# Four early sampling blocks in attention, weights by axis, denser background calls, and a second addition formed by TensorE in a four-layer image network

## The chip, the cores and the metric

The kernel runs on one core of one Trainium2 chip. The metric is the device time of one launch in microseconds (us); lower is better. Names of engines below: PE is TensorE, DVE is VectorE, ACT is ScalarE, POOL is GpSimd, SP is SyncE, which only issues DMAs here.

## The reference

The input x is 2 images of 256 channels on 64 x 64 pixels, float32. Four layers follow one another:

```
# layer 0: attention over 4096 pixels, 4 heads of 64 channels
xn = group_norm(x, groups=8)
q, k, v = split(w_qkv @ xn)
out = softmax(q^T k / 8) @ v
x = xn + w_proj @ out + b_proj
# layer 1: a position term is added
x = x + pe(W, b)
# layer 2: bottleneck with a modulated deformable 3x3 convolution on 64 channels
h = relu(bn1(w1 @ x))
off = conv3x3(h, woff) + boff            # 18 offsets and 9 masks per pixel
h = einsum(bilinear(h, y + off, x + off) * sigmoid(mask), w2)
x = relu(bn3(w3 @ relu(bn2(h))) + x)
# layer 3: two deformable 3x3 convolutions on 256 channels
h = relu(group_norm(x, groups=32))
off = pw1 @ depthwise7x7(h)              # 18 offsets per pixel
h = einsum(bilinear(h, y + off, x + off), w1)
h = relu(group_norm(h)) ; the same again with dw2, pw2, w2
return h + x
```

`bilinear` reads for each pixel and each of 9 taps the four corners around a fractional position and weighs them; the four weights are products of two weights along y and two along x.

## The kernel before, in words

All arithmetic is float32. An image is cut into 8 blocks of 512 pixels (8 rows); pixels lie on partitions, in 4 groups of 128, where samples are made. There are two large stages, `attention` and `deform`.

**The order.** The order on PE, ACT, DVE and POOL is the order in which the program issues instructions; each engine works its own list in order. SP's DMAs are issued in order as well, and one that waits for a semaphore holds those behind it. An indirect DMA (L848) is issued by POOL: 128 rows, one per partition, at addresses from an index column.

**Attention.** Four units (batch 0 heads 0-1, batch 0 heads 2-3, batch 1 likewise) of 256 counts `n`, 1024 counts in all; one turn of the main loop handles two counts: scores on PE (L580), row maxima on DVE (L592), exponentials on ACT (L598), turns on PE (L610), copies on DVE and ACT, products with v (L639). 16 counts make a `Block` of 256 query pixels. Its own steps (`compare`, `raised`, `weights`, `spread`, `combine`, `fetch`, `project`) fall due at fixed counts and run from `small(n)` and `small(n + 1)`. `combine` (L519 to L527) runs on POOL and reads the single buffer `o`, which `product` (L471, on DVE) fills again for the next block.

**Work beside attention.** `back` is a list of generators that `background(count)` advances: from unit 1 the bottleneck's first half of batch 0 (`before(0)`), from unit 2 `first_batch` (`last(0)`, `conv(0)`, then `early_image`), from unit 3 `before(1)`, put at the front, and `early_samples`. A generator that yields something true uses up one call; one that yields False gives the call to the next. There is one call at the end of each turn, and one in each `small` that has no step of its own, from unit 2 on.

`conv(b)` is the second layer of the bottleneck: 8 blocks of 18 steps. A step makes two indirect gathers (`bfour`), weighs them with four products of weights on DVE (L1067), and adds in two goes (L1077, L1078), on POOL for batch 0 and on DVE for batch 1. After 4 steps (or 2 for the ninth tap) the sums are turned on PE (L1088) and copied by ACT (L1090); `second` and `third` are its products with w2 and w3. A step uses two calls.

`early_samples` makes the first `EARLY` = 2 blocks of samples of layer 3 for batch 0 while attention still runs: `offsets` (products L805, L825, L839, then `corners`), then 36 gathers a block from the image in DRAM, each of which is stored into `samp_d` (L1261). `self.sample` does at most one store and one gather a call; the main loop calls it 11 times in 16 counts. Its buffers are tiles of attention's pools.

**Deform.** Four layers of 288 steps `s` (batch 0 and 1 of the first deformable convolution, then of the second); a block has 36 steps (9 taps x 4 groups of 128 pixels). Step s issues the gather for s + 8, and for the first `EARLY` blocks of the first layer a plain load from `samp_d` instead, on SP's queue (L1448). Steps come in two forms:

- by axis (`paired`): ACT scales two corners with one weight (`left`, L1471), DVE adds the other two (`right`, L1477), ACT scales (`first`, L1486), DVE adds (`others`, L1490). The weights are `w`, two per axis.
- by corner: ACT scales one corner (L1486), DVE adds three (three of L1496). The weights are `w4`, four per tap.

In the first layer the early blocks go by corner and the others by axis; in the other three layers every second step goes by axis.

Then PE turns the sample (L1508), ACT copies four of them (L1517), and PE multiplies with the weights (L1527). Beside it, generators are paced by `Side(start, rate, steps, more)`: it advances while its count is below rate x (s - start) + more(s). `seconds` runs `conv(1)`; `last` the offsets of the last two blocks of batch 1; `offs` the offsets of the next blocks; `images` the image of the next layer, which begins for batch 1 when `seconds` has ended.

Of the kernel before, what the change touches and what calls it, by code (L numbers as in the profile page):

```python
# [11 lines left out]
F32 = mybir.dt.float32  # L12
# [8 lines left out]
P = 128  # L21
# [3 lines left out]
CM = 64  # L25
# [1 line left out]
EPS = 1e-5  # L27
DWK = 7

EARLY = 2  # L30


GH, GW = H + 1, W + 2
# [31 lines left out]
class Net:  # L65
# [115 lines left out]
    def attention(self, bott):  # L181
# [5 lines left out]
        with ExitStack() as ctx:  # L187
# [489 lines left out]
            while n < last + 4 or back or more or any(own.values()):  # L677
                u, d = divmod(n, per_unit)
                if d == 0 and u < len(units):
                    plan_unit(u)  # L680
                    if u == 0:
                        back.append(prepare(1))
                    if u == 1:
                        back.append(bott.before(0, bt, ps))
                    if u == 2:
                        back.append(first_batch())
                    if u == 3:
                        back.insert(0, bott.before(1, bt, ps))
                        back.append(self.early_samples(bott, bt, held, xp, vp, kp, ps))

                def small(at):
                    steps = own.pop(at, ())
                    for f in steps:
                        f()
                    if not steps and u > 1:
                        background(1)

                if n - 1 in pts:
                    p = pts.pop(n - 1)
                    keep(n - 1, p, "ACT")  # L700
                    keep(n - 1, p, "DVE")
                ps.flush()
                sc = [scores(m) for m in (n + 2, n + 3) if m < last]
                for m in range(len(sc)):
                    lowest(n + 2 + m, sc[m])
                if n < last:
                    p = turn(e.pop(n))
                    keep(n, p, "DVE")
                if sc:
                    e[n + 2] = exponentials(n + 2, sc[0])  # L710
                if n < last:
                    keep(n, p, "ACT")

                small(n)
                if 4 <= n < last + 4:
                    attend(n - 4)
                    attend(n - 3)
                small(n + 1)
                if n < last:
                    pts[n + 1] = turn(e.pop(n + 1))  # L720
                if sc:
                    e[n + 3] = exponentials(n + 3, sc[1])
                if u or n % 8 == 0:
                    background(1)

                for _ in range(1 + (n % 16 in (10, 12, 14))):
                    more = self.sample()
                n += 2


    def corners(self, i, pt, mask, base, idx, w4, pool, w=None):

        nc = self.nc
        p = pool.tile([P, 4, K2, 2], F32, name="pos")
        off = pt[:, :, 0 : 2 * K2].rearrange("p j (k t) -> p j k t", t=2)
        nc.vector.tensor_tensor(p, off, base[:, 4 * i : 4 * i + 4], ALU.add)
        if mask:
            mk = pool.tile([P, 4, K2], F32, name="mask")  # L740
            nc.vector.tensor_scalar_max(mk, pt[:, :, 2 * K2 : 3 * K2], -87.0)
        yield False
        if mask:

            nc.scalar.activation(mk, mk, AF.Exp, scale=-1.0)

        nc.vector.tensor_scalar(p, p, float(H), -1.0, ALU.min, ALU.max)
        whole = pool.tile([P, 4, K2, 2], I32, name="whole")
        nc.vector.tensor_copy(whole, p)
        yield True  # L750
        f = pool.tile([P, 4, K2, 2], F32, name="floor")
        nc.vector.tensor_copy(f, whole)
        g = pool.tile([P, 4, K2, 2], F32, name="above")
        nc.vector.tensor_tensor(g, f, p, ALU.is_gt)
        yield False
        nc.vector.tensor_tensor(f, f, g, ALU.subtract)
        nc.vector.tensor_scalar_min(f, f, float(H - 1))
        if w is None:
            w = pool.tile([P, 2, 4, K2, 2], F32, name="wt")
        nc.vector.tensor_tensor(w[:, 1], p, f, ALU.subtract)  # L760
        yield False
        nc.vector.tensor_scalar(w[:, 0], w[:, 1], -1.0, 1.0, ALU.mult, ALU.add)
        at = g.rearrange("p j k t -> p (j k t)")[:, : 4 * K2]
        at = at.rearrange("p (j k) -> p j k", k=K2)
        nc.vector.scalar_tensor_tensor(
            at, f[:, :, :, 0], float(GW), f[:, :, :, 1], ALU.mult, ALU.add
        )
        nc.vector.tensor_scalar_add(idx, at, float(GW + 1))
        yield True
        if mask:  # L770
            nc.vector.tensor_scalar_add(mk, mk, 1.0)
            nc.vector.reciprocal(mk, mk)
            yield False
            for s in range(2):
                nc.vector.tensor_mul(w[:, s, :, :, 1], w[:, s, :, :, 1], mk)
            yield False
        for s in range(4):
            nc.vector.tensor_mul(w4[:, :, :, s], w[:, s % 2, :, :, 0], w[:, s // 2, :, :, 1])
        yield True

# [75 lines left out]
    class Bottleneck:  # L856
# [3 lines left out]

        GROUPS = [(0, 1), (2, 3), (4, 5), (6, 7), (8,)]

        CORNERS = NB + EARLY + 1

        def __init__(self, ctx, net):
            self.net = net
# [31 lines left out]
            self.od = wp.tile([P, 512], F32, name="bod")  # L898
            nc.gpsimd.memset(self.od, 0.0)

        def pools(self, ctx, gathers=5, sums=8):
            self.ahead = gathers - 1
            tc = self.net.tc
            return self.kept | {
                n: ctx.enter_context(tc.tile_pool(name=f"bt_{n}", bufs=bufs))
                for n, bufs in (("g", gathers), ("s", sums), ("t", 6), ("x", 2))
            }
# [135 lines left out]
        def conv(self, b, pools, ps):  # L1043
# [28 lines left out]
            def add(n, four, sampled):  # L1072

                i, g, js = steps[n]
                engine = (nc.gpsimd, nc.vector)[b]
                sm = pools["s"].tile([P, 2, CM], F32, name="bsmp")
                engine.tensor_add(four[:, :, 0:2, :], four[:, :, 0:2, :], four[:, :, 2:4, :])  # L1077
                engine.tensor_add(sm, four[:, :, 0, :], four[:, :, 1, :])  # L1078
# [5 lines left out]
            def transpose(g, sampled):  # L1084
                n = CM * len(self.GROUPS[g])
                pt = ps([P, 512])
                for j, sm in enumerate(sampled):
                    nc.tensor.transpose(pt[:n, j * P : (j + 1) * P], sm[:, :n], net.ident)  # L1088
                st = pools["t"].tile([P, 512], F32, name="bst")
                ps.later(lambda: nc.scalar.copy(st[:n], pt[:n]))  # L1090
                return st
# [122 lines left out]
                        nc.sync.dma_start(dst, t[64 * r : 64 * r + 64])  # L1214
                yield True

    def early_samples(self, bott, pools, held, xp, vp, kp, ps):


        nc, a = self.nc, self.a  # L1220
# [26 lines left out]
        for cb in range(2):  # L1247
# [2 lines left out]
            wf.append(t[:, : T * 2 * K2].rearrange("p (t o) -> p t o", o=2 * K2))  # L1250
            self.filters(wf[cb], cb, dw, pw)
            yield True
        free = deque(x.rearrange("p u n -> p (u n)") for x in xbs)
        gathers, stores = deque(), deque()

        def gather():


            if len(stores) > 1 and len(free) < 3 or not gathers and stores:
                dst, four = stores.popleft()  # L1260
                nc.sync.dma_start(dst, four)  # L1261
                free.append(four)
# [7 lines left out]
        self.sample = gather  # L1270
        for i in range(EARLY):
            idx = bott.corner.tile([P, 4, K2], I32, name="bidx")
            w4 = self.early[i] = bott.corner.tile([P, 4, K2, 4], F32, name="bw4")
            steps = self.offsets(
                i, xs,
                lambda s, row: wf[s][:, DWK * row : DWK * row + DWK, :].rearrange(
                    "p t o -> p (t o)"
                ),
                self.vec[:, V_PWB : V_PWB + 1],
                bott.base, idx, w4, pools["work"], wide, ps,  # L1280
                odp=lambda: pools["t"].tile([P, 512], F32, name="bst"), y0=rows(i)[0],
                later=ps.later,
            )
            mine = False
            for done in steps:
# [15 lines left out]
    def deform(self, bott):  # L1301
# [5 lines left out]
        with ExitStack() as ctx:  # L1307
# [90 lines left out]
                        yield  # L1398

            IMAGE = 4 + 6 * NB + 1  # L1400
            corners = {(0, 0, i): (None, w4, None) for i, w4 in self.early.items()}

            def offsets(b, l):
                if b == 0:
# [1 line left out]
                wf = self.wf  # L1406
                for i in range(EARLY if (b, l) == (0, 0) else 0, NB):
                    idx = cp.tile([P, 4, K2], I32, name="didx")
                    w4 = cp.tile([P, 4, K2, 4], F32, name="dw4")
                    w = cp.tile([P, 2, 4, K2, 2], F32, name="dwt")  # L1410
                    corners[b, l, i] = idx, w4, w
                    yield from self.offsets(
# [44 lines left out]

            def paired(s):
                n, i, _, j = parts(s)
                return s < ALL and (i >= EARLY if n == 0 else j % 2 == 1)  # L1460

            def share(s, side, axis):
                n, i, k, j = parts(s)
# [77 lines left out]
            def finish(n, i, ob, s):  # L1541
# [14 lines left out]
                        lambda: nc.vector.bn_stats(stats[b][:, ob, i, :], xs)  # L1556
                    )
                else:
                    res = work.tile([P, 512], F32, name="res")
                    nc.sync.dma_start(res, self.x2d[b][rows, cols])  # L1560

                    def second_layer():
# [18 lines left out]
                            self.steps = None  # L1581

            OFFS = 24
            inner = ExitStack()
            second = bott.conv(1, bott.pools(inner, 8, 7), ps)
            for s in range(AHEAD):
                gather(s)
# [3 lines left out]
            next(begun)  # L1591
            load(0, self.xn_d[0], wp)
            offs = [Side(EARLY * BLOCK - LEAD - 6, OFFS / BLOCK, begun)]
            first(0)


            last = Side(0, 1, bott.last(1, bott.kept, ps))
            seconds = Side(0, 0.9, second, lambda s: 2.5 * min(s, EARLY * BLOCK))
            stats[0] = self.norm_stats()
            images = []  # L1600
            for s in range(ALL + 16):
# [15 lines left out]
                if seconds:  # L1617
                    seconds.follow(s)
                    if not seconds.steps:
                        seconds = None  # L1620
                        stats[1] = bott.stats[1]
                        inner.close()
                        images.append(Side(s, 0.9, image(*layers[1])))
                if s % LAYER == LAYER // 2 and 1 <= n < len(layers) - 1:
                    images.append(
# [111 lines left out]
```

## Time and profile before

| what | value |
|---|---|
| median of 3 runs | 5122.12 us (5121.92 to 5128.18) |
| the profiled run | 5119.31 us, its span 5117.5 us, mean granted clock 0.972 |
| busy over the span | PE 4793.9 us (94%), DVE 4025.2 (79%), ACT 3251.1 (64%), POOL 2325.6 (45%) |
| indirect gathers | 1080 of `four` and 576 of `bfour` on POOL |
| stores into samp_d, loads from it | 72 and 72 of 512 KB |
| DMA | 997.68 MB, 195 GB/s over the span |
| attention | from the start to about 2985 us |
| deform | 2985 us to the end |

The page gives for each engine its busy time and, in 40 slices of 128 us, its share in tenths. A line of the groups names the source line, engine, operation, output and input, then busy time and mean duration of one, then the idle time of the engine just before these instructions and what ended it. A line of the windows gives, for a stretch of time, the busy time of PE, weight loads (PEld), DVE, ACT and POOL with counts, the granted clock of PE, the DMA share and GB/s. In a timeline the columns are start, duration, engine, line, operation and count.

### The profile page before, as it was taken

Reading aid. Unit: us, or ns where it says so; the run is one execution under the profiler, and the core shown is the slowest. Engines: PE = TensorE matmul, PEld = TensorE weight load, DVE = VectorE, ACT = ScalarE, POOL = GpSimd, SP = SyncE. Lnnn points to the kernel's source line nnn. Section 1 sums busy time; section 2 is a strip of 40 time slices with the busy share of each in tenths; the row PEclk is TensorE's granted clock in tenths of the full one; section 3 lists DMA queues with packets and bytes.
Section 4 is the critical chain, followed back from the end, with each engine's and each line's share of the span. In section 5 each row is a group of like instructions: output and inputs, shape, how many; then the busy total and the mean of one; then the engine's idle time right before and its main releaser. Section 6 shows DMA issues by size and latency. Waiting matters only on the chain. (4 is left out here: it accounts for less than half of the span.)

```text
span 5117.5 us, 100364 instructions
## 1 busy us (share of the span) xinstructions
PE 4793.9 (94%) x38200; PEld 2669.1 (52%) x38200; DVE 4025.2 (79%) x7281; ACT 3251.1 (64%) x5869; POOL 2325.6 (45%) x2256
## 2 busy tenths in 40 slices
PE   8999999999999999999999956678999999999998
PEld 5555565555565555565555523334444444444444
DVE  6878867878768888677767668867788888888888
ACT  5676656666666666666656622247876766666666
POOL 0111111111106777565123257775777666666665
PEclk9999999999999999999999977779999999999999
DMA  5231121111112333332547767679999999999998
GB/s 173 61 97 53 43 69 49 35 47 31 55 53 80 103 98 105 93 86 70 164 147 284 274 223 236 202 237 349 358 339 352 363 376 358 366 396 344 349 352 331
DMA packets 367025, 997.68 MB, mean 195 GB/s; under 512 B 61372, under 2 KB 98810, under 8 KB 366542
## 3 DMA queue, kind: packets, MB, share of 16 engines
q0 software_dynamic: 196560, 690.41, 37.4%
q1 hardware_dynamic: 169438, 300.73, 18.0%
q8 instruction: 300, 4.92, 0.4%
q14 instruction: 183, 1.50, 0.1%
q10 hardware_dynamic: 544, 0.13, 0.0%
HBM read 855.36 MB, written 127.35 MB: 192 GB/s over the span
## 5 line engine op out<-in xcount | busy, mean ns | idle before, releaser
L598 ACT ACTIVATE e<-sc,low 128x1024 f32<-128x1024 f32 x1024 | 1146.2, 1119 | 742.3 <-DVE low L592 738.0
L848 POOL DMA_INDIRECT four<-img,didx x1080 | 1152.6, 1067 | 549.9 <-issue 140.3
L592 DVE TENSOR_REDUCE low<-sc 128x1 f32<-128x1024 f32 x1024 | 1205.0, 1218 | 231.7 <-PE sc L580 227.3
L1527 PE MATMUL out<-st,wc 128*128 128x512 f32 x2304 | 1224.8, 614 | 85.7 <-ACT st L1517 41.5
L580 PE MATMUL sc<-k,qs 64*128 64x512 f32 x2048 | 999.1, 606 | 0.5 <-DVE k L368 0.3
L639 PE MATMUL av<-et,v 128*64 128x256 f32 x8192 | 997.7, 386 | 0.0
L580 PE MATMUL sc<-k,q 64*128 64x512 f32 x2048 | 978.2, 605 | 0.0
L519 POOL TENSOR_TENSOR o<-o,f 128x1024 f32<-128x1024 f32 x63 | 149.5, 2373 | 1765.2 <-DMA f<-share_d 1007.7
L610 PEld LDWEIGHTS tt<-ident,e 64*128 64x128 f32 x16384 | 655.3, 139 | 512.9 <-issue 272.7
L629 ACT COPY et<-tt 128x512 f32<-128x512 f32 x1152 | 658.4, 584 | 171.8 <-PE tt L610 170.8
L610 PE MATMUL tt<-ident,e 64*128 64x64 f32 x16384 | 728.0, 227 | 36.3 <-ACT et L629 17.7
L627 DVE COPY et<-tt 128x512 f32<-128x512 f32 x896 | 612.5, 684 | 161.5 <-PE tt L610 160.9
L1496 DVE SCALAR_TENSOR_TENSOR smp<-four,dw,smp 128x256 f32<-128x256 f32 x1296 | 627.2, 484 | 140.5 <-ACT smp L1486 109.0
L639 PEld LDWEIGHTS av<-et,v 128*64 128x64 f32 x8192 | 554.0, 137 | 300.9 <-issue 48.4
L848 POOL DMA_INDIRECT bfour<-img,bidx x576 | 584.1, 1014 | 183.9 <-issue 94.8
L1508 PEld LDWEIGHTS pt<-ident,smp 128*128 128x128 f32 x2304 | 330.5, 144 | 633.9 <-issue 470.9
L1471 ACT ACTIVATE four<-four,dwt 128x512 f32<-128x512 f32 x648 | 465.0, 718 | 200.1 <-DMA four<-img,didx 196.6
L1477 DVE SCALAR_TENSOR_TENSOR four<-four,dwt 128x512 f32<-128x512 f32 x648 | 484.9, 748 | 112.6 <-ACT four L1471 110.2
L1527 PEld LDWEIGHTS out<-st,wc 128*128 128x128 f32 x2304 | 390.9, 196 | 339.3 <-issue 222.8
L580 PEld LDWEIGHTS sc<-k,qs 64*128 64x128 f32 x2048 | 346.9, 189 | 208.7 <-issue 116.8
L1508 PE MATMUL pt<-ident,smp 128*128 128x128 f32 x2304 | 448.8, 278 | 4.6 <-DVE smp L1496 3.1
L805 PE MATMUL pd<-x,wf 128*126 128x512 f32 x840 | 436.0, 601 | 0.0
(189 smaller groups left out, 4743.1 us busy)
## 6 DMA issues: line engine op xcount, KB each, us to landing
f<-share_d SPq DMA_DIRECT2D x128, 256.0 KB
four<-samp_d SPq DMA_DIRECT2D x64, 512.0 KB
xb<-xn SPq DMA_DIRECT2D x55, 512.0 KB
img<-imgt SPq DMA_DIRECT2D x96, 256.0 KB
four<-img,didx POOLq DMA_INDIRECT x1080
xa<-res SPq DMA_DIRECT2D x32, 512.0 KB
samp_d<-xb SPq DMA_DIRECT2D x32, 512.0 KB
xb<-in_x SPq DMA_DIRECT2D x20, 512.0 KB
```

What stands on the lines that cost most here:

```text
L580: nc.tensor.matmul(s[:, j, :], lhsT=q[u, i // 2][int(h != j)][halves[j], at : at + P], rhs=k[u][c][halves[j], h, :], start=True, stop=True,)
L592: nc.vector.tensor_reduce(low, s, AX.X, ALU.max, negate=True)
L598: nc.scalar.activation(e.rearrange("p j n -> p (j n)"), s, AF.Exp, bias=blk.low[:, g, c : c + 1], accum_out=blk.sum[:, g, c : c + 1],)
L610: nc.tensor.transpose(pt[:, m, :], e[half, m // 4, m % 4 * P : m % 4 * P + P], self.ident[half, half],)
L627: nc.vector.tensor_copy(dst, pt)
L629: nc.scalar.copy(dst, pt)
L639: nc.tensor.matmul(now["av"][halves[h], :], lhsT=v[u][c][:, m, halves[h]], rhs=ets[j][:, m, h, :], start=(m == 0), stop=(m == 7),)
L848: self.nc.gpsimd.indirect_dma_start(out=dst, out_offset=None, in_=img, in_offset=bass.IndirectOffsetOnAxis(ap=idx, axis=0),)
L1477: nc.vector.scalar_tensor_tensor(uv, four[:, 2 * C :], share(s, 1, 1), uv, ALU.mult, ALU.add)
L1496: nc.vector.scalar_tensor_tensor(smps[s], four[:, c], weight(s, c), smps[s], ALU.mult, ALU.add)
L1508: nc.tensor.transpose(pts[u][:, c, j * P : (j + 1) * P], smp[:, c * P : c * P + P], self.ident,)
L1527: nc.tensor.matmul(outs[ob], lhsT=wc[k][:, c, ob * P : ob * P + P], rhs=sts[u][:, c, :], start=(k == 0 and c == 0), stop=(k == K2 - 1 and ...
```

## The change

Attention makes four early blocks instead of two, with a fifth buffer for them (the tile `pos` of attention's pool of single buffers), and the calls of `background` and `sample` come more often. The early blocks keep their weights by axis (`w` in place of `w4`), so that the whole first deform layer takes the form by axis, and its `w4` is not made. In `conv(1)` the second addition is dropped on DVE: the one addition left writes a permuted tile, and PE turns its two halves by plain products with the identity that accumulate in PSUM, where there was one transpose. The pacing of `conv(1)` in deform is 2.0 calls a step over the first 144 steps instead of 3.4 over 72. The rest makes room or follows: tiles of `corners` are shared, the pool of sums has 7 buffers instead of 8, `res` gets its pool when that of `conv(1)` has ended, and `left` and `right` of the first steps are issued ahead of the loop.

```diff
-EARLY = 2
+EARLY = 4
...
-                        background(1)
+                        background(1 + (n % 4 == 0))
...
-                for _ in range(1 + (n % 16 in (10, 12, 14))):
+                for _ in range(1 + (n % 16 in (2, 6, 10, 12, 14))):
                     more = self.sample()
...
-        whole = pool.tile([P, 4, K2, 2], I32, name="whole")
+        whole = pool.tile([P, 4, K2, 2], F32, name="whole").bitcast(I32)
...
-        g = pool.tile([P, 4, K2, 2], F32, name="above")
+        g = whole.bitcast(F32)
...
-        for s in range(4):
+        for s in range(4 if w4 is not None else 0):
             nc.vector.tensor_mul(w4[:, :, :, s], w[:, s % 2, :, :, 0], w[:, s // 2, :, :, 1])
...
-        CORNERS = NB + EARLY + 1
+        CORNERS = NB + EARLY
...
-        def pools(self, ctx, gathers=5, sums=8):
+        def pools(self, ctx, gathers=5, sums=7):
...
                 engine = (nc.gpsimd, nc.vector)[b]
+                if b == 1:
+                    sm = pools["s"].tile([P, 2, 2, CM], F32, name="bsmp")
+                    engine.tensor_add(
+                        sm.rearrange("p s n f -> p n s f"), four[:, :, 0:2, :], four[:, :, 2:4, :]
+                    )
+                    if g < 4:
+                        sampled.append(sm.rearrange("p s n f -> p s (n f)"))
+                    else:
+                        sampled.extend(sm[:, :, m, :] for m in range(2))
+                    return
...
-                    nc.tensor.transpose(pt[:n, j * P : (j + 1) * P], sm[:, :n], net.ident)
+                    dst = pt[:n, j * P : (j + 1) * P]
+                    if b == 0:
+                        nc.tensor.transpose(dst, sm[:, :n], net.ident)
+                        continue
+                    for m in range(2):
+                        nc.tensor.matmul(
+                            dst, lhsT=sm[:, m, :], rhs=net.ident, start=(m == 0), stop=(m == 1)
+                        )
...
+        xbs.append(one.tile([P, 2, 512], F32, name="pos"))
...
-            if len(stores) > 1 and len(free) < 3 or not gathers and stores:
+            if len(stores) > 1 and len(free) < 4 or not gathers and stores:
...
-            w4 = self.early[i] = bott.corner.tile([P, 4, K2, 4], F32, name="bw4")
+            w = bott.corner.tile([P, 4, K2, 4], F32, name="bw4").rearrange("p a k c -> p (a k c)")
+            w = self.early[i] = w.rearrange("p (s j k t) -> p s j k t", s=2, j=4, t=2)
...
-            corners = {(0, 0, i): (None, w4, None) for i, w4 in self.early.items()}
+            corners = {(0, 0, i): (None, None, w) for i, w in self.early.items()}
...
-                    w4 = cp.tile([P, 4, K2, 4], F32, name="dw4")
+                    w4 = cp.tile([P, 4, K2, 4], F32, name="dw4") if b or l else None
...
-                return s < ALL and (i >= EARLY if n == 0 else j % 2 == 1)
+                return s < ALL and (n == 0 or j % 2 == 1)
...
-                    res = work.tile([P, 512], F32, name="res")
+                    res = places["res"].tile([P, 512], F32, name="res")
...
+            for s in range(3):
+                left(s)
+            for s in range(2):
+                right(s)
             first(0)
...
-            seconds = Side(0, 0.9, second, lambda s: 2.5 * min(s, EARLY * BLOCK))
+            seconds = Side(0, 0.9, second, lambda s: 1.1 * min(s, EARLY * BLOCK))
...
                         inner.close()
+                        places["res"] = ctx.enter_context(tc.tile_pool(name="df_r", bufs=2))
```

More of the change, by code (lines that the diff above doesn't have):

```diff
@@ L688, in attention @@
                         back.insert(0, bott.before(1, bt, ps))
-                        back.append(self.early_samples(bott, bt, held, xp, vp, kp, ps))
+                        back.append(self.early_samples(bott, bt, held, xp, vp, kp, one, ps))
                 def small(at):
@@ L1215, in early_image, with early_samples @@
                 yield True
-    def early_samples(self, bott, pools, held, xp, vp, kp, ps):
+    def early_samples(self, bott, pools, held, xp, vp, kp, one, ps):
         nc, a = self.nc, self.a
@@ L1279, in early_samples @@
                 self.vec[:, V_PWB : V_PWB + 1],
-                bott.base, idx, w4, pools["work"], wide, ps,
+                bott.base, idx, None, pools["work"], wide, ps,
                 odp=lambda: pools["t"].tile([P, 512], F32, name="bst"), y0=rows(i)[0],
-                later=ps.later,
+                later=ps.later, w=w,
             )
@@ L1583, in deform @@
             OFFS = 24
-            inner = ExitStack()
+            inner, places = ExitStack(), {}
             second = bott.conv(1, bott.pools(inner, 8, 7), ps)
```

## The prediction

> **What bounds the kernel now.** I read part 2 of the page first, to see where TensorE is not full, then the busy times of that stage and its neighbours, then the groups inside the stage, then single instructions for prices.
>
> ```profile
> PE   8999999999999999999999956678999999999998
> POOL 0111111111106777565123257775777666666665
> PEclk9999999999999999999999977779999999999999
> ```
> Each digit is 128 us. PE is full in attention (to 2985 us) and from about 3480 us on. The hole is the opening of the deform stage, and there POOL has its highest digits.
>
> ```profile
> 1555.00:2110.00 555.00, 544.97 (x5884) 325.26 (x5882) 459.20 (x627) 373.60 (x699) 408.28 (x450) 1.00 0.33 97
> 2985.00:3484.00 499.00, 322.57 (x1002) 151.87 (x1002) 395.15 (x899) 166.26 (x294) 373.62 (x362) 0.76 0.73 240
> 3484.00:3757.00 273.00, 257.99 (x950) 129.36 (x951) 205.36 (x425) 225.22 (x392) 183.42 (x159) 0.98 0.94 351
> 3757.00:5117.00 1360.00, 1301.58 (x4746) 644.34 (x4744) 1185.25 (x2619) 927.11 (x1612) 900.51 (x856) 1.00 0.96 358
> ```
> Columns: busy PE, PEld, DVE, ACT, POOL, clock, DMA share, GB/s. Counting the one ACT scale per step (L1486: 71 by 3310, 130 by 3484, 289 by 3757), step s=128 is reached at 3484 and s=288 at 3757, so the first layer takes 772 us, 499 of them for 128 steps. The other three layers go at 1360/865 = 1.57 us a step with PE and DMA both at 96%.
>
> ```profile
> L848 POOL DMA_INDIRECT bfour<-img,bidx x288 | 299.6, 1040 | 98.6 <-issue 52.4 <-DMA bfour<-img,bidx 7.9 <-DMA x<-xn 7.2
> L848 POOL DMA_INDIRECT four<-img,didx x66 | 69.6, 1054 | 22.6 <-issue 9.1 <-DVE smp L1490 5.8 <-ACT four L1471 2.1
> L1496 DVE SCALAR_TENSOR_TENSOR smp<-four,bw,smp 128x256 f32<-128x256 f32 x216 | 104.4, 483 | 10.2 <-DMA wc<-in_dcw 4.5 <-ACT smp L1486 0.5
> L1078 DVE TENSOR_TENSOR bsmp<-bfour 128x128 f32<-128x128 f32 x143 | 41.9, 293 | 9.7 <-DVE bfour L1077 0.9
> ```
> These are the groups of 2985 to 3484. From 3060 to 3460 POOL issues 301 gathers in 400 us, one per 1.33 us: 1.04 busy, 0.3 of its own issue. 354 x 1.33 = 471 from the first at 2999 ends at 3470, 14 us before step 128. So **POOL's gathers bound the opening**; DVE is second at 79%.
>
> **Deform, part by part.** Two more blocks are 2 x 36 = 72 gathers that POOL no longer issues here; SP loads them (0.32 us of SP each, loads of the same 0.5 MB). The pacing `2.5*min(s,72)` to `1.1*min(s,144)` gives 2.0 calls a step instead of 3.4; the second convolution needs 7 + 288 calls for its last weighing, so that comes at s = 144 + 7/0.9 = 152. By then POOL has issued 288 + (152 + 9 - 144) = 305 gathers: 14 (2985 to 2999) + 305 x 1.33 (406) + 14 lag = 434 us.
>
> What else could hold those steps? DVE, from start to start:
>
> ```profile
> 3483.64 0.42 DVE L1077 TENSOR_TENSOR bfour<-bfour 128x256 f32<-128x256 f32 x1
> 3484.09 0.29 DVE L1078 TENSOR_TENSOR bsmp<-bfour 128x128 f32<-128x128 f32 x1
> 3484.30 0.74 DVE L1477 SCALAR_TENSOR_TENSOR four<-four,dwt 128x512 f32<-128x512 f32 x1
> ```
> The second addition that goes costs 0.21, the one that stays 0.45; the same stretch gives 0.60 for a weighing, 0.66 for L1477, 0.40 for each 128x256. Per step after: 0.60 + 0.45 + 0.66 + 0.40 + 0.3 (output rows, corners) = 2.4, below POOL's 2.66. Removed in all: 144 x 0.21 = 30 us, and 72 x (1.20 - 1.06) = 10 for weights by axis. ACT gains 72 x 0.72 = 52 us on 166 of 499 busy: hidden. The addition that writes a permuted tile is not in the trace; by the nearest rows it costs between 0.29 and 0.75, and I take 0.42, its size's row. The three `left` and two `right` ahead of the loop are work that moved, not added.
>
> PE gains most. Prices in the steady stage:
>
> ```profile
> 4615.69 0.38 PE L1508 MATMUL pt<-ident,smp 128*128 128x128 f32 x2
> 4615.91 1.02 PE L1527 MATMUL out<-st,wc 128*128 128x512 f32 x2
> ```
> Two turns start 0.22 before the next product, and the product's two records take 0.86. A plain product is two records, a turn one; so a turn by two products is 4 records of 128 columns. No row has exactly these: at a turn's 0.11 each 160 tiles add 160 x 3 x 0.11 = 53 us, at 0.20 (a weight load of 0.14 not quite hidden) 110. I take 0.11, as the records match in columns. PE per step: 1.08 + 1.11 x 0.44 + 0.2 (w2, w3) = 1.8, and 2.2 once the later blocks' offsets run (s over 86), at full clock; at the granted 0.76, 2.3 and 2.85. Against 2.66 this costs 66 x 0.19 = 13 if the clock stays; I take 10.
>
> The first layer then is 444 + the other 136 steps. Those took 273 for 160, and 24 steps fewer at 1.57 leaves 235: **679 against 772, 93 us less** (bounds 37 to 103).
>
> The Trainium skill's page "TensorE: Matmul & The Clock Gate", section Terms, speaks against this part: it gives the transpose mode as 4 times faster for FP32, where the rows here show two records to one. By it a turned tile would be 0.88, an estimate, 160 of them 123 us more instead of 53; the sum would be 5095, or 5165 if all of the 70 us between came through.
>
> **Attention, part by part.** Two more blocks bring their offsets:
>
> ```profile
> 2579.94 11.00 PE L805 MATMUL pm<-v,bx 128*126 128x512 f32 x28
> 2596.04 1.95 PE L825 MATMUL pm<-k,shift 126*32 126x512 f32 x14
> 2600.33 1.08 PE L839 MATMUL pm<-sel,bst 128*128 128x32 f32 x8
> ```
> 14.0 us of PE each, where PE is 98% busy: 28 us on the path. (Deform loses the same work where PE has room, so it is no gain there beyond the 93.) `load(i+1)` runs three times, not once, on SP behind stores that wait for their gathers; 72 more stores and gathers go on as long as sampling lasts. In 2580 to 2985 SP sat 227 us before the 72 stores (110+53+47+17), with attention's share and q loads behind it, and yet a count n took 2.80 us in 2640 to 2910 (193 exponentials and reads of their sums, two per count), as in the convolution before it; so I charge 8 us for both (0 to 25).
>
> **Denser calls.** In 32 counts there are 16 closing calls and 32 slots of `small`, 15 taken by own steps: 33 calls. Of the 17 free slots 7 have n%4==0: 40 calls. The work from unit 2 on (some 345 calls, shared with `before(1)` in unit 3) brings the early image from n=852 (2455 us in the trace) to about 794, and the samples from 902 to about 824. 144 samples at 13 per 16 counts take 177, so they end near n=1000 of 1028: they fit. What pays is POOL, which does the first convolution's additions too:
>
> ```profile
> 1783.35 0.73 POOL L1077 TENSOR_TENSOR bfour<-bfour 128x256 f32<-128x256 f32 x1
> 1784.16 0.45 POOL L1078 TENSOR_TENSOR bsmp<-bfour 128x128 f32<-128x128 f32 x1
> 1784.89 0.96 POOL L848 DMA_INDIRECT bfour<-img,bidx  x1 [0.27 <-POOL bsmp L1078]
> 1786.15 1.29 POOL L848 DMA_INDIRECT bfour<-img,bidx  x1 [0.30 <-issue]
> 1787.46 0.73 POOL L1077 TENSOR_TENSOR bfour<-bfour 128x256 f32<-128x256 f32 x1
> ```
> One convolution step is 4.1 us of POOL back to back (3.8 at best). Two combines (2.43+1.43+0.83) and one addition of positions are 11.8 per 32 counts. 32 counts take 555/198 x 32 = 90 us (198 exponentials in 1555 to 2110, one per count). Before: 16.5 x 4.1 + 11.8 = 79; after: 20 x 4.1 + 11.8 = 94. POOL is asked for 104%, so attention must wait for it: at least 4 us in each of 144/20 = 7.2 such stretches, 29. Behind a late combine stand DVE's next copy into `o` (one buffer, three to four counts later), behind it the row maxima, behind these ACT's exponentials and PE. I take 30; 0 if steps cost 3.8, 71 if each of 14 blocks also loses 3 us at that handover. One pool tile fewer (8 to 7) only matters where POOL is late already. The cover of the rest is PE's own work.
>
> The skill's "GPSIMD Engine Reference", Specifications, has POOL's SBUF interface shared with VectorE when that has two SBUF inputs; the gather's mean is 0.99 in 1555 to 2110 and 1.04 in the opening, where DVE does more of these. By that rule denser DVE work could bring attention's 288 gathers to 1.04, an estimate of 14 us on top.
>
> **Sum.** Attention +28 +8 +30 = +66, deform -93: -27. The profiled run took 5119.3 (span 5117.5 and 1.8 around it), 2.8 below the median of 5122.1; -27 on the median is 5095.
>
> **Rivals.** (A) POOL keeps up in attention (step 3.8: 20 x 3.8 + 11.8 = 88 of 90) and PE never shows: +36 and -103, 5055. For: POOL waited 81 us in 600 on L1067, slack the denser calls can use. Against: bursts of 5 calls in one turn. (B) The other side: POOL is what attention waits for throughout the first convolution, at 71 plus 28 plus 25 of late loads = +124 against -93: 5153; from 65 us of POOL stalls on (with 28 and nothing else) nothing is gained. For: 104%. Against: POOL that is late has no waits of its own left. (C) PE takes POOL's place in the opening: at 0.20 a record and clock 0.76 a step is 2.9, and 3.4 past s=86: 86 x 0.21 + 66 x 0.72 = 66 us, deform only -37, 5151. Against: a busier PE should not be granted 0.76. (D) The two sums cancel, 5122: the work is only moved from a stage short of POOL to a stage short of PE.
>
> **How the numbers follow.** Forecast 0.50 (own range 5070 to 5120), A 0.17, B 0.15, C 0.08, D 0.10. This kernel's runs tell 0.2% (10 us) from no change. Faster is four fifths of the forecast plus A and a little of D: 0.59; within, the forecast's rest and part of D: 0.15; slower, B, C and some of D: 0.26. Range 5045 to 5155.
>
> **What would show it.** Right: deform's opening still one gather per 1.33 us, last L1067 some 433 us after deform's start, 72 more L1448 loads; attention's end near 3050 (2985 + 66), POOL over 95% taken in 1555 to 2200, samples starting near 2400. Wrong: L471 or PE waiting on POOL for over 65 us (B); PE at 95% in the opening, its clock at 0.8 (C); attention's end under 3025 (A); samples still running after the last score would void the count.

## The result, and the profile after

The change made the kernel slower: 5189.7 us, median of 4 runs (5185.2 to 5199.6), against 5122.8 for the kernel before; the ratio is 1.013, 95% interval 1.0116 to 1.0143. The prediction was 5095, with a range to 5155. The profiled execution has a span of 5187.6 us.

The first loads from `samp_d` on POOL's queue mark the border of the two stages. They start at 2972.5 us before and 3136.5 after. So attention takes **164 us more** and deform, 2145.0 before and 2051.1 after, **94 us less**. The page of the kernel after shows the same by slices of 130 us:

```profile
PE   8999999999999999998998886788999999999998
POOL 0111111111117778740232325776677666666665
PEclk9999999999999999999999997998999999999999
```

The hole in PE is shallower and begins later, and the granted clock over the opening is 0.90 where it was 0.76; but PE's row now has eights within attention. The windows of the first convolution, the samples and the opening of deform (columns: PE, PEld, DVE, ACT, POOL, clock, DMA share, GB/s):

```profile
1546.00:2144.00 598.00, 555.33 (x5756) 325.43 (x5756) 466.47 (x634) 367.74 (x685) 446.53 (x507) 0.96 0.33 96
2735.00:3125.00 390.00, 345.75 (x3583) 204.81 (x3583) 242.47 (x391) 231.65 (x435) 111.70 (x106) 0.93 0.71 260
3149.00:3568.00 419.00, 329.96 (x1438) 188.82 (x1438) 329.72 (x670) 227.72 (x391) 318.04 (x294) 0.90 0.88 297
```

PE is busy 93% of the first stretch, where it was 98% before, and 89% of the second. Where the time goes is best read between equal counts, from the start of the exponential of each count n, one per count, taken from the timeline of ACT. The kernels of the experiments are in the same table (us between the counts):

| kernel | 512 to 768 (first convolution) | 768 to 896 | 896 to 1023 | start of deform | span |
|---|---|---|---|---|---|
| before | 740 | 386 | 383 | 2972.5 | 5117.5 |
| after | 807 | 466 | 402 | 3136.5 | 5187.6 |
| e1 calls as before | 738 | 387 | 441 | 3148.7 | 5204.3 |
| e2 11 samples | 804 | 454 | 364 | 3098.8 | 5160.1 |
| e3 deform's parts alone | 738 | 388 | 384 | 2972.2 | 5113.2 |
| e4 addition on DVE | 802 | 468 | 399 | 3131.5 | 5190.8 |
| e5 share on POOL | 805 | 451 | 343 | 3060.9 | 5109.1 |
| e6 first convolution's addition on DVE | 881 | 474 | 399 | 3216.8 | 5270.8 |
| e7 e5 and e6 | 889 | 465 | 344 | 3159.4 | 5220.5 |
| e8 e5, half as many extra calls | 756 | 463 | 345 | 3026.5 | 5080.0 |
| e9 one small addition | 764 | 465 | 399 | 3089.8 | 5148.6 |
| e11 before, share on POOL | 738 | 388 | 374 | 2962.6 | 5111.0 |

Up to count 512 all agree within 3 us. The loss of the kernel after is 67 us in the first convolution and 99 in the last unit (466 + 402 against 386 + 383). The second is where the prediction had only 36 (28 for the offsets of two blocks, 8 for all the rest).

The first convolution, from count 512 to count 768, has these windows in the kernel before, in the kernel after and in e9 (which follows below). The last line is PE's longest wait between these counts in the kernel after (who waited for whom, us in total, times, longest):

```profile
1451.90:2191.90 740.00, 728.64 (x7906) 438.05 (x7906) 581.16 (x831) 492.82 (x919) 446.14 (x489) 1.00 0.31 90
1450.90:2257.50 806.60, 759.00 (x7978) 448.67 (x7979) 605.51 (x861) 499.71 (x930) 521.12 (x585) 0.97 0.31 91
1450.60:2214.10 763.50, 739.95 (x7978) 441.88 (x7978) 599.76 (x861) 499.44 (x931) 418.41 (x455) 1.00 0.32 97
PE pm L1100 <- POOL bsmp L1088: 29.6, 14, 3.4
```

PE has only 0.9% more matmuls there than before (7978 for 7906). Of the 67 us, 36 are time in which PE is idle (48 us for 11), and 30 are longer busy time (759 for 729). Most of the idle time is one wait: at the turn of the samples (L1100) PE stands for the sum that POOL makes, 29.6 us in 14 times, where it was 0.7 us in one before. The longer busy time goes with a lower granted clock, 0.97 for 1.00: in e9 the same 7978 matmuls are busy for 740 us at 1.00.

What happens in the last unit shows in the waits of the kernel after between 2723 and 3125 us, in the form of that last line:

```profile
POOL o L519 <- DMA f<-share_d: 173.2, 7, 27.7
ACT e L598 <- DVE low L592: 107.3, 56, 12.0
...
DVE o L471 <- POOL avs L525: 52.6, 7, 11.4
```

POOL stands 25 us per block for the share `f` (before it was 23: 137.4 us in 6 times from 2580 to 2985), and DVE then stands up to 11 us for POOL's combine before it may fill `o` again. Before, this second wait was 10.4 us in 4 times. PE's longest wait in this stretch is for DVE's copies (L627): 29.9 us in 4 times, before 8.0 in 3. One block of POOL and SP in the kernel after:

```profile
2801.66 2.35 POOL L519 TENSOR_TENSOR o<-o,f 128x1024 f32<-128x1024 f32 x1 [27.68 <-DMA f<-share_d]
...
2806.29 0.97 POOL L848 DMA_INDIRECT xb<-img,bidx  x1
...
2827.30 0.94 POOL L848 DMA_INDIRECT pos<-img,bidx  x1 [2.52 <-DMA samp_d<-pos]
2850.45 2.34 POOL L519 TENSOR_TENSOR o<-o,f 128x1024 f32<-128x1024 f32 x1 [22.22 <-DMA f<-share_d]
```

```profile
2833.99 5.31 SPq L1279 DMA_DIRECT2D samp_d<-xb  x3
2841.46 0.32 SPq L1279 DMA_DIRECT2D samp_d<-pos  x1
2841.87 0.38 SPq L506 DMA_DIRECT2D share_d<-shares  x1
2845.79 1.40 SPq L510 DMA_DIRECT2D f<-share_d  x2
```

The 13 gathers of a block start after its combine, from 2806 to 2828. SP stores each sample when its gather has landed, one per 2.6 us. The share was copied by DVE at 2832.07, but its store stands behind these on SP until 2841.87; the broadcast follows at 2845.79, the combine at 2850.45, and only then the next gathers. This is a **ring**: combine, gathers, stores, share, combine. It takes 48.8 us here (2801.66 to 2850.45) and 53.6 the next time, where 16 counts of attention without it take 43 to 44. From 2735 to 3125 POOL is busy for 29% and DMA for 71%. But the DMA share is uneven within a turn of the ring: 0.95 from 2806 to 2842, while the samples move, and 0.30 from 2842 to 2858, while share and broadcast go.

### The profile page after: what moved, and what is told of

The parts are those of the page before. It is cut to its first block, busy times and chain, and to the rows that moved or that the text cites. A ratio compares the mean times of both kernels' runs of the same rounds, so it can differ in the third digit from the quotient of the medians.

```text
span 5187.6 us, 101488 instructions
## 1 busy us (share of the span) xinstructions
PE 4849.8 (93%) x38680; PEld 2717.7 (52%) x38680; DVE 3958.2 (76%) x7033; ACT 3302.5 (64%) x5941; POOL 2323.0 (45%) x2256
## 5 line engine op out<-in xcount | busy, mean ns | idle before, releaser
L848 POOL DMA_INDIRECT four<-img,didx x1008 | 1067.3, 1059 | 525.3 <-issue 132.0
L1546 PE MATMUL out<-st,wc 128*128 128x512 f32 x2304 | 1209.9, 607 | 78.0 <-ACT st L1536 41.8
L639 PE MATMUL av<-et,v 128*64 128x256 f32 x8192 | 1021.6, 393 | 0.0
L627 DVE COPY et<-tt 128x512 f32<-128x512 f32 x896 | 612.9, 684 | 147.7 <-PE tt L610 147.1
L848 POOL DMA_INDIRECT bfour<-img,bidx x576 | 601.4, 1044 | 182.2 <-issue 97.1
L1490 ACT ACTIVATE four<-four,dwt 128x512 f32<-128x512 f32 x576 | 413.5, 718 | 141.7 <-DMA four<-img,didx 138.6
L1496 DVE SCALAR_TENSOR_TENSOR four<-four,dwt 128x512 f32<-128x512 f32 x576 | 431.1, 748 | 81.3 <-ACT four L1490 79.8
L805 PE MATMUL pd<-x,wf 128*126 128x512 f32 (+2 forms) x784 | 395.5, 586 | 0.2 <-DVE wf L784 0.2
```

The costliest lines, as they stand in the source:

```text
L627: nc.vector.tensor_copy(dst, pt)
L639: nc.tensor.matmul(now["av"][halves[h], :], lhsT=v[u][c][:, m, halves[h]], rhs=ets[j][:, m, h, :], start=(m == 0), stop=(m == 7),)
L805: nc.tensor.matmul(pd[:m, r0 * W : r1 * W], lhsT=wt(s, t), rhs=src[:, (y + r0 - y0) * W : (y + r1 - y0) * W], start=(n == 0), stop=(n == l ...
L848: self.nc.gpsimd.indirect_dma_start(out=dst, out_offset=None, in_=img, in_offset=bass.IndirectOffsetOnAxis(ap=idx, axis=0),)
L1546: nc.tensor.matmul(outs[ob], lhsT=wc[k][:, c, ob * P : ob * P + P], rhs=sts[u][:, c, :], start=(k == 0 and c == 0), stop=(k == K2 - 1 and ...
```

## The experiments

**e1, the calls.** One extra background call taken back:

```diff
-                        background(1 + (n % 4 == 0))
+                        background(1)
```

> The kernel after with one background call per free slot, as before; all else stays. Theory 1 (denser calls ask POOL for more than it has during the first convolution): count 768 is reached near 2192 us as before, not 2258, a gain of 66 us there. The samples then start near count 902 and only 126/16 x 13 = 102 of 144 fit into attention; the other 42 follow it at 2.6 us each, 110 us, so the whole is 5190 - 66 - 19 (fewer counts beside samples) + 110 = 5215 us. Rival (the early blocks' offsets and samples cost attention its time, the calls nothing): count 768 stays at 2258 and the whole is near 5300.

Measured: 5203.0 us, 12 below theory 1's 5215, ratio 1.0157 (1.014 to 1.0174). The 67 us of the first convolution are gone (738), and the samples that no longer fit run on after the last count, from 3018 to about 3148. So the denser calls alone cost what is lost between 512 and 768. With the four blocks' offsets now between 896 and 928, as in the kernel before, these 32 counts take 148 us where two blocks make it 120: 28 us for two blocks' offsets.

**e2, the samples.** The pace of samples as before:

```diff
-                for _ in range(1 + (n % 16 in (2, 6, 10, 12, 14))):
+                for _ in range(1 + (n % 16 in (10, 12, 14))):
```

> The kernel after with 11 sample calls per 16 counts instead of 13. Theory 1 (a ring: stores into samp_d wait on SP for their gathers, the share of a block waits behind them, POOL's combine waits for the share, the next gathers wait behind the combine; 13 samples at 2.6 us plus 17 us of share and combine are 51 us per 16 counts, 11 are 45.5): 32 counts beside samples take 91 us instead of 101, attention ends 40 to 50 us earlier, and some 5 samples are left after the last count: 5145 to 5160 us in all. Rival (each sample costs attention the same, whenever it is made): the pace per sample stays, within 10 us of 5190.

Measured: 5162.4, ratio 1.0079 (1.0062 to 1.0096). Counts 896 to 1023 take 364 us instead of 402, 92 per 32 instead of 101. That is theory 1's pace, and a total 2 us above its range. The cost depends on how dense the samples are, not on how many there are.

**e3, deform's parts alone.** The kernel after with

```diff
-EARLY = 4
+EARLY = 2
...
-                        background(1 + (n % 4 == 0))
+                        background(1)
...
-                for _ in range(1 + (n % 16 in (2, 6, 10, 12, 14))):
+                for _ in range(1 + (n % 16 in (10, 12, 14))):
...
-            seconds = Side(0, 0.9, second, lambda s: 1.1 * min(s, EARLY * BLOCK))
+            seconds = Side(0, 0.9, second, lambda s: 2.5 * min(s, EARLY * BLOCK))
```

> Two early blocks, calls, samples and pacing of the second convolution as before; what stays of the change is weights by axis in the whole first layer and the second addition formed by PE. Theory 1 (POOL's gathers bound the opening of deform): nothing for POOL changes, 5122 us, within 10; DVE loses some 40 us of work in the opening. Rival 1 (DVE's work bound it as much): up to 40 us faster, 5082. Rival 2 (the turns by two products hold PE back): slower by up to 60, 5180.

Measured: 5121.3 against 5121.5, ratio 1.0004 (0.9994 to 1.0013). The window of the opening, by the same columns:

```profile
2985.00:3484.00 499.00, 355.73 (x1467) 206.52 (x1468) 333.76 (x670) 210.06 (x362) 375.67 (x361) 0.84 0.71 239
```

DVE lost 61 us of work (395 to 334), more than the 40 expected, PE gained 33, POOL stayed at 376, and the time did not move. With the gathers unchanged, freeing DVE is worth nothing here.

**e4, the second addition back on DVE.** The two branches by `b` in `add` and `transpose` take batch 0's form for both batches:

```diff
-                if b == 1:
+                if False:
...
-                    if b == 0:
+                    if True:
```

> The kernel after with both additions of the second convolution on DVE and one transpose per tile, as before. Theory 1 (POOL bounds the opening at 2.66 us a step, DVE would need 2.6): 5190 to 5200 us. Rival (PE's four records per tile cost what the clock and the waits make of them): faster by 13 to 60 us, 5130 to 5177. Second rival (DVE, not POOL, is what the opening waits for): slower by 30, 5220.

Measured: 5188.9 against 5189.7 for the kernel after; ratio to before 1.0131 (1.0114 to 1.0148). Whether DVE or PE forms that sum makes no difference to the whole with four early blocks either. Between the profiled executions deform is 8 us longer in e4 (2059.4 for 2051.1) and attention 5 us shorter.

**e5, the share off SP's queue.** In the last unit:

```diff
-                    nc.sync.dma_start(d, t)
+                    queue = nc.gpsimd if self.u == 3 else nc.sync
+                    queue.dma_start(d, t)
...
-                        nc.sync.dma_start(
+                        queue.dma_start(
                             self.f[halves[h]], src.unsqueeze(0).to_broadcast([64, 4, 256])
```

> The kernel after, but in the last unit the share of a block and its broadcast go by POOL's queue instead of SP's, so that they no longer stand behind the stores into samp_d. Theory 1 (the ring store - share - combine - gather paces attention beside the samples): 32 counts take 90 us from count 864 on instead of 101, and attention ends 40 to 60 us earlier: 5130 to 5150 us. Rival (the samples' traffic of 1 MB each slows attention's own DMAs or the engines whatever the queue): still 101 per 32 counts, 5190 or, with POOL's waits for the share, up to 5210.

Measured: 5115.9, 74 us faster than the kernel after, ratio to before 0.9988 (0.9978 to 0.9997). The gain is larger than expected: 896 to 1023 fall to 343 us, 87 per 32 counts, which is faster than the 92 beside 11 samples in e2. POOL in this kernel:

```profile
2800.38 0.54 POOL L507 DMA_DIRECT2D share_d<-shares  x1 [10.06 <-DVE shares L504]
2804.65 1.09 POOL L511 DMA_DIRECT2D f<-share_d  x2 [3.73 <-DMA share_d<-shares]
2806.04 1.00 POOL L849 DMA_INDIRECT xb<-img,bidx  x1 [0.30 <-issue]
...
2809.58 2.37 POOL L520 TENSOR_TENSOR o<-o,f 128x1024 f32<-128x1024 f32 x1
...
2841.45 0.55 POOL L507 DMA_DIRECT2D share_d<-shares  x1 [11.89 <-DVE shares L504]
```

The share leaves as soon as DVE has made it (POOL waits for DVE, not the other way), the combine follows 9 us later without a wait, and the period is 41 us. SP still waits as long for its gathers, but attention's share no longer stands behind it. The samples' traffic is the same, and the DMA share is now 0.95 over a whole cycle (2800.4 to 2841.4), where the ring's cycle (2801.66 to 2850.45) had 0.83. So neither the amount of traffic nor POOL's time was the cause, but what waited for what. Of the 59 us won from count 896 to 1023, 20 are busy time of PE: the same 3712 matmuls take 337 us at a granted clock of 1.00, where the kernel after has 357 at 0.93.

**e6, POOL relieved by DVE.** The second addition of the first convolution:

```diff
-                engine.tensor_add(sm, four[:, :, 0, :], four[:, :, 1, :])
+                nc.vector.tensor_add(sm, four[:, :, 0, :], four[:, :, 1, :])
```

> The kernel after, but the second addition of the first convolution is on DVE instead of POOL. Theory 1 (POOL is asked for 94 us in 90): a step costs POOL 4.1 - 0.73 = 3.4 us, 80 of 90; counts 512 to 768 take 740 to 760 us instead of 807, and the whole is 5125 to 5145 us. Rival (the denser calls crowd DVE and PE, not POOL): DVE gets 144 x 0.29 = 42 us more in that stretch, which then takes 807 or more: 5190 to 5230 us.

Measured: 5277.8, ratio 1.0304 (1.0287 to 1.0321); 881 us where the kernel after takes 807. This looks like the rival, but the waits between 1546 and 2144 tell of something else:

```profile
DVE bsmp L1088 <- POOL bfour L1087: 121.3, 65, 6.1
POOL bfour L848 <- DVE bsmp L1088: 112.3, 92, 4.1
POOL bfour L1087 <- DVE bfour L1067: 105.7, 36, 30.0
```

Each step now passes from DVE to POOL and back to DVE, and the next gather, behind on POOL, waits for DVE too. DVE stood still for POOL (121 us) with attention's work behind it. From count 512 to 768 DVE is busy for 633 of 881 us (72%), in the kernel after for 606 of 807 (75%): it wasn't crowded. So the trial doesn't decide between the two theories, since its edit makes a wait of its own.

**e7, e5 and e6 together.**

> Both of the last two together. Theory 1: the gains add, as they lie in different counts: 5190 - 50 - 55 = 5085 us, below the kernel before by some 35. Rival (one wait takes the place of the other; DVE is late in both stretches): 5130 to 5190 us.

Measured: 5215.6, ratio 1.0178 (1.0161 to 1.0195). 889 us from count 512 to 768 (881 in e6) stand beside 344 from 896 on (343 in e5): the two stretches are nearly independent, and most of e5's gain holds (62 us against e6, 74 alone). Theory 1's 5085 fails by the loss of e6.

**e8, half as many extra calls.** On top of e5:

```diff
-                        background(1 + (n % 4 == 0))
+                        background(1 + (n % 8 == 0))
...
-                for _ in range(1 + (n % 16 in (2, 6, 10, 12, 14))):
+                for _ in range(1 + (n % 16 in (2, 6, 8, 10, 12, 14))):
```

> The share on POOL's queue as in e5, the extra background call at every eighth count instead of every fourth (36.5 calls in 32 counts instead of 40), and 14 samples per 16 counts instead of 13 so that 144 fit from count 850 on. Theory 1 (POOL's time per 32 counts: 18.25 x 4.1 + 11.8 = 87 of 90): counts 512 to 768 take 740 to 755 us instead of 805, samples end near count 1015, the whole is 5116 - 55 = 5060 us (5050 to 5075). Rival (bursts of double calls, not POOL's mean, hold attention): half of the 66 us stays, 5085; or, if denser samples bring the ring back, 5100 and more.

Measured: 5079.3, ratio to before 0.9913 (0.9900 to 0.9927), 43 us faster than the kernel before and 110 faster than the kernel after. The first convolution takes 756 us, 16 above before instead of 67, 1 us beyond theory 1's range; and 14 samples per 16 counts, with the share out of SP's queue, run at the pace of 13. PE's wait for POOL's sums at the turn is down to 4.8 us in 2 times. The total is 4 us above the expected range.

**e9, POOL's time alone.** The first addition is dropped, and with it two of the four corners, so that POOL is relieved and no other engine gets work for it:

```diff
-                engine.tensor_add(four[:, :, 0:2, :], four[:, :, 0:2, :], four[:, :, 2:4, :])
-                engine.tensor_add(sm, four[:, :, 0, :], four[:, :, 1, :])
+                engine.tensor_add(sm, four[:, :, 0, :], four[:, :, 2, :])
```

> The kernel after, where the first convolution leaves out two of its four corners: one addition of 128x128 on POOL instead of two, nothing put elsewhere; calls, weighing, turns and gathers stay. Theory 1 (POOL's time): a step costs POOL 3.4 us, 20 x 3.4 + 11.8 = 80 of 90, and counts 512 to 768 take 740 to 750 us instead of 807; 5125 to 5135 in all. Rival (the denser calls' work on DVE and PE): 800 us and 5185.

Measured: 5148.9, ratio 1.0053 (1.0034 to 1.0071), 764 us between 512 and 768. POOL's groups between 1546 and 2100 (busy, mean ns, idle before):

```profile
L848 POOL DMA_INDIRECT bfour<-img,bidx x233 | 228.9, 982 | 66.1 <-issue 35.0 <-POOL bsmp L1087 24.9 <-DVE et L627 2.4
L1087 POOL TENSOR_TENSOR bsmp<-bfour 128x128 f32<-128x128 f32 x117 | 56.8, 485 | 144.3 <-DVE bfour L1067 105.9 <-PE pm L1099 20.8 <-PE tt L610 13.1
```

43 of the 67 us come back, as theory 1 has it, though 764 is 14 beyond its range. From count 512 to 768 PE's wait for POOL's sums falls from 29.6 us to 5.1, its idle time in all from 48 to 24, and its busy time by 19 us as the granted clock is 1.00 again. Of the 24 that stay, 11 are PE's busy time (740 us for 729 before, with 72 matmuls more) and 12 its other idle time. POOL now waits 106 us for DVE's weighing, but it did so for 70 us in the kernel after too (1546 to 2144), so this wait alone does not tell that POOL has room. That the 12 us come of the calls' bursts, up to 5 in one turn, is argued and not shown.

**e11, the ring in the kernel before.** The edit of e5 in the kernel before:

> The kernel before with only the share of a block and its broadcast on POOL's queue in the last unit. Theory 1 (the ring binds where it is longer than the 44 us that 16 counts take: 11 samples make it 45.5, 13 make it 51): a small gain over the 102 counts of samples, 5 to 15 us: 5107 to 5117. Rival (the share's place in SP's queue costs attention as much without the change, so that e5's 74 us are a gain of their own and no loss of the change): 40 us or more, below 5085.

Measured: 5112.8 against 5123.8, ratio 0.998 (0.9971 to 0.9989). An 11 us gain with 11 samples per 16 counts: the ring was already touching attention's pace before the change, and the two samples more per 16 counts put some 2.4 us each on it (101 us per 32 counts in the kernel after, 92 in e2).

## Why the prediction was wrong, point by point

**POOL's gathers bound the opening, and two more early blocks take 93 us off deform: right.** Deform lost 93.9 us, and e3 and e4 show that DVE's work and the form of the turns were worth 8 us there at most. The last weighing of the second convolution comes at about step 152, as forecast, and starts 454 us after deform's first load. The prediction counted from 2985, 12.5 us behind that load; from there it is 442 us, against 434 and 10 for PE. That the two agree is in part luck: a gather cost 1.10 us of POOL, not 1.04, and came one per 1.40 us (215 in the 300 us from 3250) instead of 1.33, so the gathers took 428 us instead of 406, while the 14 us of lag behind them and the 10 for PE did not show.

**PE's four records per turned tile at 0.11 each: right, and without weight.** Sixteen records go by in 1.88 us, 0.1175 each:

```profile
3299.83 2.05 PE L1103 MATMUL pm<-ident,bsmp 128*128 128x128 f32 x16 [0.52 <-DVE bx L1140]
3301.71 1.02 PE L1546 MATMUL out<-st,wc 128*128 128x512 f32 x2
```

The 0.88 us a tile that followed from the fourfold price of the Trainium skill (page "TensorE: Matmul & The Clock Gate", section Terms) is 0.47 here. Rival C falls: PE is busy 79% of the opening at clock 0.90.

**Permuted addition at 0.42: right** (mean 418 ns).

**Two blocks' offsets, 28 us on attention's path: right** (e1: 148 against 120 us for the same counts).

**Denser calls, 30 us (0 to 71): the engine right, the path and the size wrong.** They cost 67. The prediction let the loss go by a late combine, DVE's copy into `o`, the row maxima and ACT; but from count 512 to 768 DVE waits at L471 for POOL for only 0.3 us. PE itself stood for POOL's sums at the turn, and its busy time grew with the lower clock. 43 us hang on POOL's addition (e9), of which the sum over 7.2 stretches saw 29 to 30; the 24 that remain without it were not in the sum at all.

**"So I charge 8 us for both (0 to 25)": this step failed.** It took the pace beside 11 samples, 2.80 us a count, as proof that SP's 227 us of waiting hid behind PE's work. But the ring was already part of that pace: e11 gains 11 us by opening it. The last unit takes 769 us before and 868 after. Of the 99 us between, 28 are the offsets of two blocks (e1). e5, without the ring, takes 794, 74 less than the kernel after; the same edit wins 7 in the kernel before (762 in e11), so some 67 of the 99 are the ring, in place of the 8. The last 4 are open. The rows for it were in view: 13 samples at 2.6 us and some 17 us of share, broadcast and combine are 51 us, more than the 44 that 16 counts take. The queue was named, with the share behind its waiting stores, but who waited for the share, and that the next stores waited for that, was not followed round.

67 + 99 is the 164 us of attention to within 2 us, and 164 - 94 is the 70 us of the spans. Rival B, attention waiting for POOL, came nearest. Its sign, L471 or PE waiting on POOL for over 65 us, came true (52.6 us beside the samples, 29.6 in the first convolution), and its 71 for the first convolution is near the 67 measured. But it had 25 us for late loads where the ring took 67; so it ended at 5153 and the kernel at 5190.

## What to carry to other kernels

When transfers that wait are put on an in-order queue, follow who waits for what stands behind them until the chain ends or closes on itself; a closed chain has a period, and each item more in it is added to the time almost in full once that period passes the loop's own. An unchanged pace under a long queue wait proves no slack: the wait can already be at the limit, and moving the one small transfer off that queue tests it. When a full engine's work is to be spread, a chain of steps that alternates between two in-order engines can cost more than it frees.

## What the runs showed of the hardware that was not expected

- The price of a gather on POOL varies, and DVE's load alone does not tell it: a mean of 1040 ns in the opening before (DVE busy for 79%), 1043 in e3 (67%), 1102 after (79%), 1135 in e4 (87%). The opening after:

```profile
L848 POOL DMA_INDIRECT bfour<-img,bidx x283 | 311.8, 1102 | 96.2 <-issue 55.8 <-DVE smp L1509 12.8 <-DMA bfour<-img,bidx 7.9
```

  The kernel after against e4 fits DVE's load; before against after does not. The DMA share of the opening also rose, from 0.73 to 0.88, but the last three layers have 1048 ns at 0.96. The cause is open. In the first convolution the gather stayed at 986 ns (990 before), so the estimate that the prediction worked out for that stage from the Trainium skill (page "GPSIMD Engine Reference", section Specifications) did not come true.
- Turning by products instead of transposes went with a higher granted clock of PE: in the opening 0.76 before and 0.84 in e3, with two early blocks, and 0.84 in e4 and 0.90 after, with four. The Trainium skill (page "TensorE: Matmul & The Clock Gate", Part 4) has it that the full clock does not engage for transposes, which don't count as busy in the same way; that fits, but PE was also busy for 33 us more in e3 and 36 more in the kernel after, so the runs don't separate the two. The time of the whole did not change with it.
- In attention PE's idle time and its granted clock moved together, so a wait cost more than its length. From count 512 to 768 PE was idle for 11 us at a clock of 1.00 before and for 48 at 0.97 after; from 896 to 1023 for 44 us at 0.93 after and for 6 at 1.00 in e5. The same matmuls took 19 us more busy time in the kernel after than in e9, and 20 more than in e5.
